# Adding a causal mask in the PSUM bank: identity matmuls on the tensor engine in place of some vector additions

## The chip, the cores and the metric

One core of one Trainium2 chip runs the whole program in one launch. The metric is the device time of one execution, in microseconds (us); the time of a kernel is the median over its runs. All data are float32.

## The reference

The input x holds 8 sequences of 1024 tokens with 256 features. Two layers run over each sequence:

```
x  = x + causal_attention(layernorm(x)) + top1_of_8_experts(layernorm(x))     # layer 0
xn = layernorm(x)
x  = x + attention_on_log_map(xn) + butterfly_ffn(xn)                         # layer 1
```

Both attentions have 16 heads of 16 features. The layer-0 attention is causal:

```python
scores = jnp.einsum('bhki,bhqi->bhkq', k, q) / math.sqrt(HS)
mask = jnp.arange(n)[:, None] <= jnp.arange(n)[None, :]
scores = jnp.where(mask, scores, jnp.float32(NEG_INF))      # NEG_INF = -10000.0
prob = jax.nn.softmax(scores, axis=2)
combined = jnp.einsum('bhkq,bhkl->bhql', prob, v)
```

The layer-1 attention has no mask. The rest (router and experts of layer 0, log map, dynamic metric, butterfly transforms and GELU of layer 1) is not touched here.

## The kernel before

**Naming.** The causal attention of sequence n is called a*n*, the layer-1 attention b*n*; the tiles carry the letter (mx_a, mx_b). The attentions are computed in the order a0, a1, b0, a2, b1, a3, ... a7, b6, b7. An attention is four groups of four heads, and a group has two halves h of 512 query tokens. In a group each head owns a strip of 32 rows of the array, so a score matmul has a contraction of 32 rows and occupies a quarter of the array; the two pairs of heads are called pr = 0 and pr = 1, the two heads of a pair j = 0 and 1.

**Two passes over the scores.** The softmax needs the maximum of each query's row before the exponentials.

- *First pass*, `max_step`: the tensor engine computes scores with the queries on the partitions (L441) into a tile of two PSUM banks, one bank for each head of the pair. The vector engine (DVE) takes the maximum of each row (L455). In a causal attention some 128x128 blocks lie on the diagonal; there DVE first adds `negmask` (0 at and below the diagonal, -1e30 above it) to the scores in the bank (L451). `maxima` (L464 to L475) joins the parts of a half, and `put_max` transposes the negated maxima (L481, tensor engine) and adds them into a free row of the query tile, so that the second pass subtracts them within its matmul.
- *Second pass*, `exp_step` and `weigh`: scores with the keys on the partitions (L504, tensor engine), exponentials (L512, ACT), zeros above the diagonal (L516, POOL), then the products with the values (av, L526, tensor engine, full 128 rows). `norm_out` and `norm` (from L537) divide by the sum, after transposes (tile ut).

**The causal first pass of a group.** A half has, for each pr, one *wide* item with two diagonal blocks (a part 384 wide and a part 128 wide, side by side in the bank) and two *narrow* items with one diagonal block (512 and 256 wide); the second half has four more items without a diagonal. So a group has 4 wide and 8 narrow items with a mask, and the 8 causal attentions have 32 groups, hence 384 additions at L451.

**The order of the work** is written out by a program that runs when the kernel is built; the engines take their instructions in that order. Each step of the main loop issues, for each pr, an `exp_step` of the current group, then as many items of the first pass of a later group as a quota by due time asks for (first the items of the other pr, whose strips of the array are free, so that L441 and L504 run side by side), then the `weigh` of an earlier step, the `norm` and `put_max` that are due, and then fill work. The fill work (projections, router, experts, metric, butterflies, the folded feed-forward with L391 and L1201, layer norms) is given out by a scheduler (`Fill`) from hand-written lanes by planned costs and due times. The planner does not count the time of the mask addition or of anything in `max_step`.

**PSUM.** The tiles of both passes, the transposed maxima (nm) and ut share one ring of three tiles of two banks each (`pair_bank`); av has one bank, the fill work one more.

**Constants.** `ident` (128x128 identity) and `negmask` lie in one constant tile (cst in the profile), both from the host.

Of the kernel before, what the change touches and what calls it, by code (L numbers as in the profile page):

```python
# [18 lines left out]
P = 128  # L19
# [182 lines left out]
def two_layers(ctx: ExitStack, tc: tile.TileContext, a: dict, out: bass.AP):  # L202
# [14 lines left out]
    PE, DVE, ACT, POOL, SP = nc.tensor, nc.vector, nc.scalar, nc.gpsimd, nc.sync  # L217
# [13 lines left out]
    def pair_bank(name):  # L231
        return ps_sc.tile([P, 2, 512], F32, tag="sc", name=name)
# [22 lines left out]
    ident = cst[:, C_ID : C_ID + P]  # L255
    negmask = cst[:, C_NEG : C_NEG + P]
# [29 lines left out]
    for s, tag in enumerate(("gm", "h", "wst", "wst", "second", "xT1", "vT")):  # L286
        bufs = 1 if tag in ("gm", "second", "xT1", "vT") else None
        t = work.tile([P, 2048], F32, tag=tag, name=f"paths_{s}", **({"bufs": bufs} if bufs else {}))
# [34 lines left out]
    for i in range(2):  # L323
        t = const.tile([P, NT, 8, 3, 16], F32, tag=f"vals{i}", name=f"vals{i}")
# [4 lines left out]
    for par in range(2):  # L329
        t = const.tile([P, 4, P], F32, tag=f"negmax{par}", name=f"negmax{par}")  # L330
# [72 lines left out]
    class Attention:  # L403
# [29 lines left out]
        def max_step(self, g, parts, pr):  # L433

            qT, kT, mm = self.q[g], self.k[g], self.mm[g]
            sc = pair_bank(f"mx_{self.n}_{g}_{parts[0][0]}_{parts[0][1]}_{pr}")
            at = [0, parts[0][2]]
            for (t, k, w), o in zip(parts, at):
                for j in range(2):
                    r = 32 * (2 * pr + j)  # L440
                    PE.matmul(  # L441
                        sc[:, j, o : o + w], qT[r : r + 32, t * P : (t + 1) * P],
                        kT[r : r + 32, k * 512 : k * 512 + w], start=True, stop=True,
                    )
            t, k, w = parts[0]
            if self.causal and k * 512 + w == (t + 1) * P:
                shape = [P, 2, len(parts), P]
                own = sc[:, :, w - P : w - P + len(parts) * P].rearrange(
                    "p j (i f) -> p j i f", f=P
                )  # L450
                DVE.tensor_tensor(  # L451
                    own, own, negmask.unsqueeze(1).unsqueeze(1).to_broadcast(shape), ALU.add
                )
            for (t, k, w), o in zip(parts, at):
                DVE.tensor_reduce(  # L455
                    mm[:, t, 2 * pr : 2 * pr + 2, k], sc[:, :, o : o + w], AX.X, ALU.max
                )
# [1138 lines left out]
```

## Time and profile before

| what | value |
|---|---|
| time, median of 3 runs | 4759.27 us (4754.95, 4759.27, 4760.77) |
| profiled execution, own time | 4754.35 us |
| its span | 4752.6 us |
| mean clock granted to the tensor engine | 0.989 |
| busy: tensor engine (PE) | 4596.2 us |
| busy: its weight loads (PEld, beside PE) | 1935.5 us |
| busy: DVE | 3049.0 us |
| busy: ACT | 2206.8 us |
| busy: POOL | 740.8 us |

The profile is one execution as the hardware profiler recorded it. Its span runs from the first to the last instruction; the device time adds 1.75 us. A group line gives line of the kernel, engine, operation, out<-in tiles, their shapes, how many; then busy us, the mean of one in ns, the idle time of the engine just before these instructions, and what ended it. A float32 matmul leaves two records on the tensor engine (and two weight loads), so 2048 matmuls stand as x4096. The end of a matmul is modelled, and matmuls overlap in the pipeline: their mean duration is longer than the distance from one to the next. The chain of waits follows the last instruction back to what released it, step by step. The granted clock is the share of full speed that the tensor engine was given.

In the profile the first pass of a0 lies from 24 to 266 us, that of a1 from 276 to 530 us. Groups 2 and 3 of a2 lie from 1026 to 1144 us, those of a3 from 1610 to 1723, a4 from 2188 to 2300, a5 from 2765 to 2878, a6 from 3343 to 3456 and a7 from 3922 to 4031 us.

### The profile page before, as it was taken

The page shows a single profiled execution, that of the slowest core. Times are in us where ns is not written, and L with a number is a line of the kernel's source. Part 1 is how long each engine was busy: PE and PEld are TensorE (multiplying, and loading weights), DVE is VectorE, ACT ScalarE, POOL GpSimd, SP SyncE. Part 2 cuts the span into 40 slices and gives each one's busy share as a digit, 9 for nine tenths or more (in the row PEclk, how much of TensorE's full clock was granted, in tenths as well). Part 3 has the DMA queues.
Part 4 walks back from the last instruction along what each step waited for, and adds up shares of the span by engine and source line. Part 5 has one row for each costly group of instructions (what it writes and reads, how often), then busy time and mean ns, then how long its engine had stood idle before and what let it go on. Part 6 is the DMA issues. An engine that isn't in the chain of part 4 may idle for free.

```text
span 4752.6 us, 68497 instructions
## 1 busy us (share of the span) xinstructions
PE 4596.2 (97%) x27808; PEld 1935.5 (41%) x27808; DVE 3049.0 (64%) x4926; ACT 2206.8 (46%) x2813; POOL 740.8 (16%) x1213
## 2 busy tenths in 40 slices
PE   7989999999999999999999999999999999999998
PEld 3444443344433444344443444434443344433332
DVE  6777565666566765667656676566675666666554
ACT  2443445544454444544445444454445544454544
POOL 4233202021020210202121021211112011010000
PEclk8899999999999999999999999999999999999999
DMA  4121101020001100012000110001100011000000
GB/s 166 55 66 54 54 3 34 23 67 21 13 25 34 61 18 15 26 34 67 7 27 18 34 62 8 27 22 48 46 6 28 28 40 37 15 10 10 1 10 10
DMA packets 85692, 158.24 MB, mean 33 GB/s; under 512 B 12672, under 2 KB 67584, under 8 KB 82176
## 3 DMA queue, kind: packets, MB, share of 16 engines
q1 hardware_dynamic: 69632, 89.88, 5.7%
q0 software_dynamic: 15744, 63.98, 4.3%
q8 instruction: 219, 3.59, 0.3%
q14 instruction: 97, 0.79, 0.1%
HBM read 117.25 MB, written 36.57 MB: 32 GB/s over the span
## 4 chain that ended last, share of the span: by engine, by line
PE 87%; DVE 7%; ACT 3%; issue 1%; DMA 0%; POOL 0%; POOLq 0%; DVEq 0%; SPq 0%; ACTq 0%
PE sc_b L504 19%; PE av_b L526 10%; PE sc_a L504 9%; PE mx_b L441 6%; PE av_a L526 5%; PE w L1201 5%; PE f L391 5%; PE mx_a L441 4%; PE g_b L1127 2%; PE e L842 2%; DVE mm_a L455 2%; PE h_b L391 2%; ACT p_b L512 2%; PE k_a L391 1%; PE q_b L391 1%
## 5 line engine op out<-in xcount | busy, mean ns | idle before, releaser
L455 DVE TENSOR_REDUCE mm_b<-mx_b 128x2 f32<-128x1024 f32 x1024 | 1249.6, 1223 | 769.6 <-PE mx_b L441 769.1
L512 ACT ACTIVATE p_b<-sc_b 128x1024 f32<-128x1024 f32 x1024 | 1043.0, 1022 | 1184.5 <-PE mx_b L441 740.7
L441 PE MATMUL mx_b<-kT_b,qT_b 32*128 32x512 f32 x4096 | 1144.6, 638 | 10.9 <-ACT p_b L512 10.6
L504 PE MATMUL sc_b<-qT_b,kT_b 32*128 32x512 f32 x4096 | 1142.7, 638 | 9.3 <-ACT p_b L512 6.9
L512 ACT ACTIVATE p_a<-sc_a 128x1024 f32<-128x1024 f32 (+1 forms) x640 | 598.5, 937 | 740.2 <-PE sc_a L504 392.7
L455 DVE TENSOR_REDUCE mm_a<-mx_a 128x2 f32<-128x1024 f32 (+3 forms) x768 | 722.7, 955 | 254.4 <-PE mx_a L441 239.5
L441 PE MATMUL mx_a<-kT_a,qT_a 32*128 32x512 f32 (+3 forms) x3072 | 673.4, 535 | 22.1 <-DVE mm_a L455 15.9
L504 PE MATMUL sc_a<-qT_a,kT_a 32*128 32x512 f32 (+3 forms) x3072 | 679.3, 533 | 8.3 <-ACT p_a L512 5.4
L504 PEld LDWEIGHTS sc_b<-qT_b,kT_b 32*128 32x128 f32 x4096 | 308.7, 183 | 619.7 <-issue 429.9
L526 PE MATMUL av_b<-p_b,vals 128*32 128x512 f32 x4096 | 548.9, 605 | 0.6 <-ACT p_b L512 0.6
L516 POOL TENSOR_SCALAR_AFFINE_SELECT p_a<-p_a 128x256 f32<-128x256 f32 (+1 forms) x384 | 189.4, 493 | 1388.2 <-ACT p_a L512 1387.9
L504 PEld LDWEIGHTS sc_a<-qT_a,kT_a 32*128 32x128 f32 x3072 | 247.0, 186 | 345.5 <-issue 235.1
L441 PEld LDWEIGHTS mx_b<-kT_b,qT_b 32*128 32x128 f32 x4096 | 307.5, 183 | 63.8 <-ACT p_b L512 49.5
L526 PE MATMUL av_a<-p_a,vals 128*32 128x512 f32 (+3 forms) x3072 | 321.3, 507 | 0.0
L451 DVE TENSOR_TENSOR mx_a<-mx_a,cst 128x256 f32<-128x256 f32 (+1 forms) x384 | 198.5, 517 | 174.3 <-PE mx_a L441 131.4
L441 PEld LDWEIGHTS mx_a<-kT_a,qT_a 32*128 32x128 f32 x3072 | 245.2, 187 | 102.6 <-ACT p_a L512 22.8
L1201 PE MATMUL w<-wcon,f 128*128 128x256 f32 x1024 | 260.1, 392 | 3.1 <-ACT f L1193 3.1
L826 POOL DMA_INDIRECT ew<-in_ew,rows_a x120 | 116.7, 973 | 850.3 <-PE mx_b L441 508.6
L526 PEld LDWEIGHTS av_b<-p_b,vals 128*32 128x32 f32 x4096 | 81.1, 108 | 382.3 <-issue 373.6
L1201 PEld LDWEIGHTS w<-wcon,f 128*128 128x128 f32 x1024 | 183.0, 189 | 119.1 <-issue 83.3
L391 PE MATMUL f<-xT_b,wexp 128*128 128x512 f32 x512 | 223.9, 595 | 0.0
L526 PEld LDWEIGHTS av_a<-p_a,vals 128*32 128x32 f32 x3072 | 68.2, 110 | 214.9 <-issue 173.0
(227 smaller groups left out, 4202.9 us busy)
## 6 DMA issues: line engine op xcount, KB each, us to landing
ew<-sorted_d SPq DMA_DIRECT2D x120, 128.0 KB, 2.1
mixed_d<-res SPq DMA_DIRECT2D x120, 128.0 KB, 1.7
x<-in_x SPq DMA_DIRECT2D x8, 1024.0 KB, 5.7
wexp<-wexp_d SPq DMA_DIRECT2D x8, 1024.0 KB, 4.8
wcon<-wcon_d SPq DMA_DIRECT2D x8, 1024.0 KB, 5.4
paths<-in_paths SPq DMA_DIRECT2D x7, 1024.0 KB, 13.3
out<-x SPq DMA_DIRECT2D x7, 1024.0 KB, 4.4
w<-in_w1t SPq DMA_DIRECT2D x8, 512.0 KB, 3.8
```

Of the source, the lines that this page charges most:

```text
L391: PE.matmul(ps, w[:, c, cols : cols + P], rhs[:, c, h * 512 : (h + 1) * 512], start=(c == 0), stop=(c == 1),)
L441: PE.matmul(sc[:, j, o : o + w], qT[r : r + 32, t * P : (t + 1) * P], kT[r : r + 32, k * 512 : k * 512 + w], start=True, stop=True,)
L451: DVE.tensor_tensor(own, own, negmask.unsqueeze(1).unsqueeze(1).to_broadcast(shape), ALU.add)
L455: DVE.tensor_reduce(mm[:, t, 2 * pr : 2 * pr + 2, k], sc[:, :, o : o + w], AX.X, ALU.max)
L504: PE.matmul(sc[:, j, o : o + 512 - c0], kT[r : r + 32, kt * P : (kt + 1) * P], qT[r : r + 32, h * 512 + c0 : (h + 1) * 512], start=True, s ...
L512: ACT.activation(p[:, :, lo:], sc[:, :, lo:], AF.Exp, scale=0.25)
L516: POOL.affine_select(own, own, [[0, 2], [0, n], [1, P]], ALU.is_ge, 0.0, base=0, channel_multiplier=-1,)
L526: PE.matmul(av[32 * i : 32 * i + 32, c0:], self.vals[:, kt, 4 * (g // 2) + i, odd : odd + 2, :].rearrange("p e d -> p (e d)"), p2[i // 2][ ...
L826: POOL.indirect_dma_start(halves[:, s % 2, : 3 * D], None, a["ew"], bass.IndirectOffsetOnAxis(ap=rows[:, s : s + 1], axis=0),)
L842: PE.matmul(ps[:, :D], was[:, c * P : (c + 1) * P], w[:, c * D : (c + 1) * D], start=(c == 0), stop=(c == 1),)
L1127: PE.matmul(ps, w2t[:, m, c * P : (c + 1) * P], hT[:, m, :], start=(m == 0), stop=(m == 3),)
L1201: PE.matmul(ps[:, :D], hT[k // 4][:, k % 4, i * P : (i + 1) * P], wcon[:, k, :], start=(k == 0), stop=(k == 7),)
```

## The change

For all groups of the sequences 0 and 1, and for the groups 2 and 3 of the sequences 2 to 7 (20 of the 32 causal groups), the mask is no longer added by DVE. The score matmul leaves its accumulation open, and for each head j and each diagonal block one more matmul, of `ident` (stationary, 128x128) with `negmask` (moving, 128 columns), adds the mask to the block in the bank: two such matmuls for a narrow item, four for a wide one. They use all 128 rows of the array, in float32 like the others. The groups 0 and 1 of the sequences 2 to 7 keep the addition on DVE. The maximum (L455) is taken as before.

```diff
@@ max_step
             at = [0, parts[0][2]]
+            t, k, w = parts[0]
+            masks = self.causal and k * 512 + w == (t + 1) * P
+            added = masks and (self.b < 2 or g > 1)
             for (t, k, w), o in zip(parts, at):
                 for j in range(2):
                     r = 32 * (2 * pr + j)
                     PE.matmul(
                         sc[:, j, o : o + w], qT[r : r + 32, t * P : (t + 1) * P],
-                        kT[r : r + 32, k * 512 : k * 512 + w], start=True, stop=True,
+                        kT[r : r + 32, k * 512 : k * 512 + w], start=not (o and added), stop=not added,
                     )
             t, k, w = parts[0]
-            if self.causal and k * 512 + w == (t + 1) * P:
+            if added:
+                for j in range(2):
+                    for o in range(w - P, w - P + len(parts) * P, P):
+                        PE.matmul(
+                            sc[:, j, o : o + P], ident, negmask, start=False,
+                            stop=o == w - P + (len(parts) - 1) * P,
+                        )
+            elif masks:
                 shape = [P, 2, len(parts), P]
                 own = sc[:, :, w - P : w - P + len(parts) * P].rearrange(
                     "p j (i f) -> p j i f", f=P
```

## The prediction

> **What bounds the kernel now.** I read the page first, then the chain of waits, then stretches of time, then the groups of the shapes that the change touches, then single moments of the timeline. The page's head and its chain:
>
> ```profile
> span 4752.6 us, 68497 instructions
> ...
> PE 4596.2 (97%) x27808; PEld 1935.5 (41%) x27808; DVE 3049.0 (64%) x4926; ACT 2206.8 (46%) x2813; POOL 740.8 (16%) x1213
> ...
> PE 87%; DVE 7%; ACT 3%; issue 1%; DMA 0%; POOL 0%; POOLq 0%; DVEq 0%; SPq 0%; ACTq 0%
> ```
>
> The tensor engine has work 97% of the time and carries 87% of the chain. A change that moves work from DVE to it starts with a loss, unless it hits the places where DVE is what ends last (7% of the chain, some 330 us). So I asked for the stretches in which the touched mask additions (L451) lie. The first pass of sequences 0 and 1 ends by 560 us; groups 2 and 3 of the sequences 2 to 7 lie in six stretches of about 130 us. Columns: stretch, its length, busy us and instructions of each engine, clock granted to the tensor engine, share of the DMA engines, GB/s.
>
> ```profile
> 0.00:560.00 560.00, 495.22 (x3026) 234.63 (x3028) 414.66 (x840) 220.40 (x322) 176.38 (x282) 0.94 0.25 81
> 1010.00:1140.00 130.00, 122.91 (x754) 55.56 (x752) 84.67 (x159) 54.25 (x67) 24.78 (x45) 0.95 0.15 47
> 1590.00:1720.00 130.00, 123.65 (x792) 55.79 (x788) 88.16 (x166) 56.35 (x69) 25.23 (x47) 0.97 0.14 44
> 2168.00:2298.00 130.00, 123.65 (x803) 55.84 (x795) 89.60 (x169) 56.73 (x70) 25.57 (x48) 0.99 0.14 44
> 2745.00:2875.00 130.00, 123.66 (x794) 55.91 (x788) 88.64 (x166) 56.29 (x69) 25.09 (x47) 0.97 0.14 44
> 3323.00:3453.00 130.00, 122.88 (x796) 55.75 (x788) 88.63 (x166) 56.29 (x69) 25.25 (x47) 0.99 0.14 44
> 3902.00:4032.00 130.00, 125.52 (x814) 56.95 (x812) 84.69 (x148) 57.08 (x70) 23.91 (x47) 1.00 0.11 36
> ```
>
> These 1340 us hold 1237.5 us of tensor work: 102.5 of the 156 us that this engine idles in the whole run are here. 21 of them no mask can touch (13.8 at the start, 7.2 behind one long DVE wait at 37 us). The missing clock is worth another 51 us (0.06 x 560 plus 0.05, 0.03, 0.01, 0.03 and 0.01 x 130). So 81 + 51 = 132 us is what the array loses here to waits and to the half clock that follows them. One such place in the chain, 1066 to 1076 us (start, us, what):
>
> ```profile
> by line: DVE mm_a L455 20.7%; DVE mx_a L451 13.9%; issue 9.9%; PE nm_a L481 8.4%; PE sc_a L504 7.5%; DVE st_a L353 6.6%; DVE on_a L577 4.3%; PE mx_a L441 4.2%; DVE es_a L572 4.2%; DVE mv_a L354 3.6%; DVE negmax L473 3.6%; DVE vals L605 3.3%
> ...
> 1073.26 0.60 DVE mx_a L451
> 1073.86 0.02 issue
> 1073.88 1.30 DVE mm_a L455 x2
> 1075.18 0.14 issue
> 1075.32 0.84 PE nm_a L481 x4
> ```
>
> For 8 us the chain runs on DVE without a break, and the transposes of L481 wait for it.
>
> **What the change removes.** The order of the instructions on ACT, POOL and SP is the same; DVE loses 240 rows, the tensor engine gains 240 groups, and nothing else moves. So the scheduler's plan stays, and the change does what it says.
>
> ```profile
> L451 DVE TENSOR_TENSOR mx_a<-mx_a,cst 128x256 f32<-128x256 f32 x256 | 109.6, 428 | 96.3 <-PE mx_a L441 59.4 <-PE sc_a L504 27.1 <-PE sc_b L504 8.4
> L451 DVE TENSOR_TENSOR mx_a<-mx_a,cst 128x512 f32<-128x512 f32 x128 | 88.9, 695 | 78.0 <-PE mx_a L441 72.0 <-issue 3.0 <-ACT junk_b L1021 2.3
> ```
>
> There are 12 additions in a group (8 narrow, 4 wide), 20 of the 32 groups change: 160 x 0.428 + 80 x 0.695 = 124 us off DVE. How much of it lies on the path? I cut the chain into the seven stretches and read L451's share: 3.9% of the first 560 us (21.8 us) and 3.8 to 4.9% of about 100 us in each of the six (27.5 us together). That is 49 us of the 124, or 39%. The other 61% ran beside tensor work and is worth nothing.
>
> **What it adds.** A narrow item gets two identity matmuls, a wide one four. Each fp32 matmul leaves two records (L441: 2048 for sequences b stand as x4096), so 160 x 4 + 80 x 8 = 1280 records, each 128 columns with a full 128x128 weight load. No such record exists now. The nearest are two moments of the timeline and a group of another shape:
>
> ```profile
> 3594.28 0.30 PEld L684 LDWEIGHTS rank_a<-hot_a,cst 128*128 128x128 f32 x2 [0.76 <-issue]
> 3594.50 0.30 PEld L685 LDWEIGHTS rank_a<-hot_a,ones 128*128 128x128 f32 x2
> 3594.72 1.60 PEld L1201 LDWEIGHTS w<-wcon,f 128*128 128x128 f32 x8
> ```
>
> ```profile
> L391 PE MATMUL f<-xT_b,wexp 128*128 128x512 f32 x512 | 223.9, 595 | 0.0
> ```
>
> Two records of 64 columns follow each other every 0.22 us, 0.11 each. 512 columns cost 223.9 / 512 = 0.437, so 128 columns stream in 0.109. Both ways a record costs 0.11: 1280 x 0.11 = 141 us. A change between full-array and tiled matmuls costs about 0.09 more (L771's neighbour at 2010.41 takes 0.52 until the tiled L504, two records of 256 columns stream in 0.437). In the changed order 140 of the 240 groups stand before a tiled matmul (104 before av, 24 before another mx, 12 before sc), the rest before full-array ones, which only get the change of shape that the mx block pays today: 13 us. Together 154. Bounds: 141 without any such cost; halfway between the 64-column record and the 256-column one of L1201 (260.1 / 1024 = 0.254, so about 0.16), 1280 x 0.16 + 13 = 218. I take 154, since two rows agree on 0.11. It can't be below nothing: the array does these columns in addition.
>
> A rule is weighed here. The Trainium skill, TensorE: Matmul & The Clock Gate, section Back-to-back issue gap, gives about 81 ns for a matmul of 128 columns in a stream of loads and matmuls. By it the records would cost 1280 x 0.081 = 104 us, an estimate from that page, and the whole would end 50 us earlier; the rows above have no full-array record under 0.11.
>
> **What hides.** The identities wait for nothing new: they follow their own item in the same bank. Behind them stand av, the fill work and the next scores, all 0.44 or 0.88 us later. The maximum (L455) now waits for the last identity in place of the addition; 0.44 takes the place of 0.43 and 0.88 that of 0.70, so the bank comes free about when it did where DVE is not late. Where the chain runs on DVE (39% of the touched time) the array waits anyway, and the identities fit in: 0.39 x 154 = 60 us hidden, 94 left. There DVE also gets shorter by 49 us; what is late next is the array itself, with its longer item, so I count two thirds, 33 us. The clock: fewer idle microseconds leave the array at half speed less often; a tenth of 51, 5 us. Sum: 94 - 33 - 5 = +56. Recovered in all: 98 of the 132 us that are there, so I would not go higher.
>
> A second rule speaks against this change: Perfetto Trace Analysis, section Identifying the Most-Contended Engine, says to relieve the engine that is used most, and also that busy matmul time does not measure headroom and the share of weight loads does. By its second half the array, at 41% of weight loads, has room for all 154 us and only DVE's relief would show, 4721 us. The stretches speak against that: the idle time and lost clock there are 132 us, not 59% of 1340.
>
> The profiled execution took 4754.35 us by its own time, 1.75 more than its span; the median of the three runs is 4759.27, 4.9 above. 4754.35 + 56 + 4.9 = 4815.
>
> **The rivals.** *DVE decides the stretches.* The array cools and idles there because DVE is late; the identities fill that time and keep the clock up. All 132 us come back against 141, and DVE's 33 stand: 4754 - 24 = 4730. For it: in 120 to 140 and 160 to 190 us DVE is over 90% busy, the clock under 0.8 in places. Against: even there the chain gives L451 only 39% of its own time. It wins once over 116 us (154 - 33 - 5), three quarters of the identities, are hidden. Chance 0.19. *Nothing hides.* In-order identities push av and the next scores even where DVE was late, and DVE then waits for the array: +154 to +218, 4908 to 4972. For it: 97% busy. Against: the chain above. Chance 0.08. *A draw*, the gain and the loss within 0.2% (9.5 us, about what a measurement of this kernel can tell from no change): 0.07.
>
> **How the numbers follow.** The forecast, slower by 10 to 145 us, has 0.66. Upper end: price 218, 39% of it hidden, 133 left, and little relief, 4890; a piece of the second rival takes it to 4900. Lower end: price 141, hidden 55, the full 49 and half of the clock (25) gives +12; to leave out no more than 2 in 10 the range must reach into the first rival, 4745. Slower 0.66 + 0.08, same 0.07, faster 0.19.
>
> **What would show it.** Right: the new line at about 0.11 us a record, 141 us of full-array work; DVE busy down by 124 to about 2925 us; tensor busy time up by more than the span; idle time and lost clock in the seven stretches down by about 60 to 100 us; sequences' other stretches unchanged in length. Wrong: a record at 0.16 or more; clock and idle time unchanged (then nothing hid); or the stretch 0 to 560 shorter by over 30 us and the six others not longer (then DVE was the bound).

## The result and the profile after

The changed kernel takes 4818.06 us (median of 4 runs, 4812.29 to 4818.78) against 4760.02 us before (4 runs): a ratio of 1.0119, interval 1.0107 to 1.0132. The forecast was 4815 us. The profiled execution has an own time of 4818.13 us.

The page's engine row and chain by engine of the changed kernel:

```profile
span 4816.4 us, 70587 instructions
...
PE 4711.1 (98%) x29088; PEld 2064.1 (43%) x29088; DVE 2927.0 (61%) x4686; ACT 2208.7 (46%) x2813; POOL 740.2 (15%) x1213
...
PE 93%; DVE 3%; ACT 3%; issue 1%; DMA 0%; POOL 0%; POOLq 0%; DVEq 0%; SPq 0%; ACTq 0%
```

DVE is 122 us shorter and its share of the chain falls from 7% to 3%; the tensor engine's rises from 87% to 93%. Its busy time grew by 115 us, the span by 64: its idle time fell by 51.

The group of the identities (line moved to L452) and, from the chain by line, what carries the stretch of groups 2 and 3 of a3, before (1590.53 to 1721.02 us) and after (1617.86 to 1752.80 us; L504, L526, L441 and L455 are now L514, L536, L444 and L465):

```profile
L452 PE MATMUL mx_a<-cst 128*128 128x128 f32 x1280 | 208.4, 296 | 0.0
```

```profile
by line: PE sc_a L504 21.1%; PE av_a L526 11.7%; PE f L391 10.7%; PE mx_a L441 8.3%; issue 7.5%; DVE mm_a L455 5.3%; PE v_b L1087 4.1%; PE k_a L391 3.0%; DVE mx_a L451 2.9%; PE w L1201 2.8%; PE q_a L391 2.8%; ACT p_a L512 2.4%; PE e L842 2.
```

```profile
by line: PE sc_a L514 25.7%; PE av_a L536 14.7%; PE mx_a L452 12.9%; PE mx_a L444 10.7%; PE f L391 10.3%; PE v_b L1097 5.1%; PE k_a L391 2.9%; PE e L852 2.7%; PE w L1211 2.7%; PE q_a L391 2.7%; ACT p_a L522 2.3%; PE nm_a L491 1.7%; PE q_b L
```

Before, `mm_a` and `mx_a` on DVE had 8.2% of this chain; after, they are not among the lines shown, and the identities have 12.9%. Next, the stretches that the prediction showed, each cut at the same ACT instructions in both traces; columns as there. Before, then after, for the first stretch, the one of a3 and the one of a7:

```profile
0.00:559.04 559.04, 494.26 (x3020) 234.50 (x3024) 413.70 (x839) 219.44 (x321) 176.38 (x282) 0.94 0.25 80
1590.53:1721.02 130.49, 124.14 (x788) 55.72 (x781) 88.68 (x166) 56.34 (x69) 25.07 (x46) 0.97 0.14 44
3902.51:4031.82 129.31, 124.83 (x806) 56.59 (x803) 84.05 (x146) 56.90 (x70) 23.75 (x46) 1.00 0.11 37
```

```profile
0.00:579.24 579.24, 542.70 (x3532) 288.86 (x3536) 362.24 (x743) 220.11 (x321) 175.96 (x282) 0.97 0.24 78
1617.86:1752.80 134.94, 133.22 (x907) 67.03 (x900) 77.84 (x144) 56.53 (x69) 25.07 (x46) 1.00 0.13 43
3955.36:4094.99 139.63, 137.39 (x927) 69.08 (x920) 72.85 (x123) 57.06 (x69) 23.75 (x46) 1.00 0.10 34
```

The first stretch is 20.2 us longer, the six late ones 35.5 us together (3.9, 4.4, 6.1, 4.8, 6.0 and 10.3), the others 8 us together; these hold the few identities that lie past the cuts (each late stretch holds 120 to 125 of its 128 records). The stretch of a7 pays most. Before, it had the least to give: 4.5 us idle, clock 1.00, while that of a3, for one, had 6.4 us idle and a clock of 0.97.

Two places of the timeline of the changed kernel (start, us, what) show the price of a group:

```profile
1049.28 1.16 PE L452 MATMUL mx_a<-cst 128*128 128x128 f32 x8
1050.37 1.14 PE L444 MATMUL mx_a<-kT_a,qT_a 32*128 32x384 f32 x8
...
1116.45 0.71 PE L452 MATMUL mx_a<-cst 128*128 128x128 f32 x4
1117.10 1.06 PE L536 MATMUL av_a<-p_a,vals 128*32 128x512 f32 x8
```

Eight records hold the array for 1.09 us, four for 0.65. In the starts of all records the pattern is the same: the first record of a group lasts 0.213 us to the next start, the others 0.111 to 0.112, and the last 0.205 where a tiled matmul follows. Summed over the 240 groups that is 180 us: 1280 x 0.1115 = 143, 240 x 0.10 = 24 for the first records, 140 x 0.093 = 13 for the last ones.

Not all of it is added. A full-array matmul that follows a tiled one has a longer first record too, and loses this when a group of identities stands before it. One place in the changed kernel, then the same place in a kernel of the next section that has no mask there:

```profile
1051.44 1.16 PE L452 MATMUL mx_a<-cst 128*128 128x128 f32 x8
1052.43 1.03 PE L1097 MATMUL v_b<-wv,vT_b 128*128 128x256 f32 x4
```

```profile
1002.70 1.14 PE L444 MATMUL mx_a<-kT_a,qT_a 32*128 32x128 f32 x10
1003.77 1.13 PE L1097 MATMUL v_b<-wv,vT_b 128*128 128x256 f32 x4
```

The four records of L1097 take 1.03 us behind identities and 1.13 behind scores. Over the 100 groups that stand before a full-array matmul these differences sum to about 8 us. So the identities add 172 us of array time. (Taken from the starts at all 240 places in the two kernels, the difference is 169.)

### The profile page after: what moved, and what is told of

Its sections match the earlier page's. It is cut to its first block, busy times and chain, and to the rows that moved or that the text cites. A ratio compares the mean times of both kernels' runs of the same rounds, so it can differ in the third digit from the quotient of the medians.

```text
span 4816.4 us, 70587 instructions
## 1 busy us (share of the span) xinstructions
PE 4711.1 (98%) x29088; PEld 2064.1 (43%) x29088; DVE 2927.0 (61%) x4686; ACT 2208.7 (46%) x2813; POOL 740.2 (15%) x1213
## 4 chain that ended last, share of the span: by engine, by line
PE 93%; DVE 3%; ACT 3%; issue 1%; DMA 0%; POOL 0%; POOLq 0%; DVEq 0%; SPq 0%; ACTq 0%
PE sc_b L514 19%; PE sc_a L514 10%; PE av_b L536 10%; PE mx_b L444 6%; PE av_a L536 6%; PE w L1211 5%; PE f L391 5%; PE mx_a L444 4%; PE mx_a L452 4%; PE g_b L1137 2%; PE e L852 2%; PE h_b L391 2%; ACT p_b L522 2%; PE v_b L1097 1%; PE k_a L391 1%; PE q_b L391 1%
## 5 line engine op out<-in xcount | busy, mean ns | idle before, releaser
L465 DVE TENSOR_REDUCE mm_b<-mx_b 128x2 f32<-128x1024 f32 x1024 | 1249.2, 1222 | 772.0 <-PE mx_b L444 765.6
L444 PE MATMUL mx_b<-kT_b,qT_b 32*128 32x512 f32 x4096 | 1144.7, 638 | 11.4 <-ACT p_b L522 11.2
L514 PE MATMUL sc_b<-qT_b,kT_b 32*128 32x512 f32 x4096 | 1142.6, 638 | 9.2 <-ACT p_b L522 6.8
L465 DVE TENSOR_REDUCE mm_a<-mx_a 128x2 f32<-128x1024 f32 (+3 forms) x768 | 722.0, 954 | 519.1 <-PE mx_a L452 265.3
L444 PE MATMUL mx_a<-kT_a,qT_a 32*128 32x512 f32 (+3 forms) x3072 | 670.0, 527 | 6.9 <-ACT p_a L522 5.5
L514 PE MATMUL sc_a<-qT_a,kT_a 32*128 32x512 f32 (+3 forms) x3072 | 664.8, 524 | 2.5 <-ACT p_a L522 1.3
L514 PEld LDWEIGHTS sc_b<-qT_b,kT_b 32*128 32x128 f32 x4096 | 308.7, 183 | 619.6 <-issue 431.6
L536 PE MATMUL av_b<-p_b,vals 128*32 128x512 f32 x4096 | 548.9, 605 | 0.6 <-ACT p_b L522 0.6
L526 POOL TENSOR_SCALAR_AFFINE_SELECT p_a<-p_a 128x256 f32<-128x256 f32 (+1 forms) x384 | 189.4, 493 | 1457.5 <-ACT p_a L522 1457.2
L514 PEld LDWEIGHTS sc_a<-qT_a,kT_a 32*128 32x128 f32 x3072 | 242.0, 183 | 332.9 <-issue 255.7
L444 PEld LDWEIGHTS mx_b<-kT_b,qT_b 32*128 32x128 f32 x4096 | 307.6, 183 | 66.0 <-ACT p_b L522 51.7
L536 PE MATMUL av_a<-p_a,vals 128*32 128x512 f32 (+3 forms) x3072 | 315.7, 498 | 0.0
L444 PEld LDWEIGHTS mx_a<-kT_a,qT_a 32*128 32x128 f32 x3072 | 243.6, 184 | 72.2 <-ACT p_a L522 21.7
L536 PEld LDWEIGHTS av_b<-p_b,vals 128*32 128x32 f32 x4096 | 81.1, 108 | 382.4 <-issue 373.6
L452 PE MATMUL mx_a<-cst 128*128 128x128 f32 x1280 | 208.4, 296 | 0.0
L452 PEld LDWEIGHTS mx_a<-cst 128*128 128x128 f32 x1280 | 162.4, 192 | 103.5 <-issue 91.1
```

The costliest lines, as they stand in the source:

```text
L444: PE.matmul(sc[:, j, o : o + w], qT[r : r + 32, t * P : (t + 1) * P], kT[r : r + 32, k * 512 : k * 512 + w], start=not (o and added), stop ...
L452: PE.matmul(sc[:, j, o : o + P], ident, negmask, start=False, stop=o == w - P + (len(parts) - 1) * P,)
L465: DVE.tensor_reduce(mm[:, t, 2 * pr : 2 * pr + 2, k], sc[:, :, o : o + w], AX.X, ALU.max)
L514: PE.matmul(sc[:, j, o : o + 512 - c0], kT[r : r + 32, kt * P : (kt + 1) * P], qT[r : r + 32, h * 512 + c0 : (h + 1) * 512], start=True, s ...
L526: POOL.affine_select(own, own, [[0, 2], [0, n], [1, P]], ALU.is_ge, 0.0, base=0, channel_multiplier=-1,)
L536: PE.matmul(av[32 * i : 32 * i + 32, c0:], self.vals[:, kt, 4 * (g // 2) + i, odd : odd + 2, :].rearrange("p e d -> p (e d)"), p2[i // 2][ ...
```

## The experiments

Three explanations give the same sum. **The prediction's**: the identities partly fit into idle time that DVE makes, and DVE's relief gives something besides. **Rival A**: nothing is hidden, and all that comes back is DVE's relief. **Rival B**: the relief is worth nothing, and identities lie in idle time. Each result is compared with the kernel before as it ran on the same chip; it took 4761.7 us there in the runs of the first four, 4749.8 in those of the next four, 4761.8 in those of the last two.

**The price alone.** The addition is kept beside the identities.

```diff
-            elif masks:
+            if masks:
```

> The selected groups get the identity matmuls and keep the addition on DVE as well (the mask is added twice, which changes no maximum of an unmasked score). This shows the price of the identities with DVE not relieved. The prediction's split (154 us of tensor work, 60 of them hidden in idle time that DVE makes, 38 us relief): 4760 + 94 = 4854, 4840 to 4870. Rival A, nothing is hidden and the whole recovery is DVE's relief: 4760 + 154 = 4914, 4900 to 4930. Rival B, DVE's relief is worth nothing and the identities lie in idle time: as with the change, 4818, 4810 to 4830.

Measured: 4865.04, +103 us, ratio 1.0212 (1.0196 to 1.0228). This lies in the prediction's range; A and B are both out. Of the 172 us of added array time 69 took no time, although DVE did as much as before. Taking the addition away from there gives 103 - 58 = 45 us.

**The relief alone.** The mask is left out of the first pass in the selected groups: no identities, no addition (the score matmul closes its accumulation as before), so the maximum is taken over masked scores too and is only an upper bound.

```diff
-            if added:
+            if False:
 ...
-            elif masks:
+            elif masks and not added:
```

> The selected groups get no mask at all in the first pass, neither identities nor addition, so the maximum is taken over the masked scores of the diagonal blocks too. This shows DVE's relief alone. The prediction's split: 4760 - 38 = 4722, 4711 to 4727. Rival A (all of the recovery, 98 us, is relief): 4662, 4650 to 4675. Rival B (relief is worth nothing): 4760, 4750 to 4765.

Measured: 4684.67, -77 us, ratio 0.9832 (0.9817 to 0.9847). All three were wrong: the relief is twice what the prediction gave it, though less than A's. So the parts don't add: +103 and -77 make +26, and both together +58. The other 32 us are time that the identities and the relief both claim, as the table below shows. The first stretch and that of a3 in this kernel:

```profile
0.00:529.78 529.78, 477.86 (x3020) 228.57 (x3024) 365.51 (x744) 219.13 (x322) 176.80 (x282) 0.97 0.26 85
1557.22:1678.74 121.52, 118.63 (x788) 53.85 (x781) 77.72 (x144) 56.54 (x70) 25.53 (x46) 1.00 0.15 47
```

With the same tensor instructions the first stretch is 29 us shorter than before and that of a3 9 us. Idle time and lost clock (1 less the granted clock, times the length; the clock is shown in two digits, so this is good to some 3 us; idle time at half clock, 6 us before and 1 in the change, counts in both columns) over the seven stretches:

| kernel | idle | lost clock |
|---|---|---|
| before | 102.5 | 50.4 |
| identities and addition | 65.7 | 28.4 |
| neither (the relief alone) | 72.8 | 15.9 |
| the change | 50.9 | 17.4 |
| identities twice | 48.3 | 7.7 |

The identities beside the addition bring back 59 of the 153 us in the two columns, the relief alone 64, the change 85: 38 are claimed by both. The relief alone brings 30 us of idle time and 34 of clock. Clock is nearly half of its worth, and the chain of waits doesn't name it under DVE: it shows as longer matmuls (the same 3020 records of the first stretch are busy for 494 us before and 478 without the mask). The tensor engine's waits for `mm_a` on DVE, all of them, before and in the changed kernel (us in total, times, longest):

```profile
PE mx_a L441 <- DVE mm_a L455: 15.9, 22, 1.3
PE ut_a L564 <- DVE mm_a L455: 7.2, 8, 0.9
PE nm_a L481 <- DVE mm_a L455: 5.5, 5, 1.1
PE sc_a L504 <- DVE mm_a L455: 1.5, 4, 0.6
```

```profile
PE mx_a L444 <- DVE mm_a L465: 1.3, 3, 0.7
```

That is 30.1 us before and 1.3 after; without a mask it is 7.4, and with identities and addition 7.6.

**Early and late apart.**

```diff
-            added = masks and (self.b < 2 or g > 1)
+            added = masks and self.b < 2                  # early
+            added = masks and self.b > 1 and g > 1        # late
```

> Identities only in the sequences 0 and 1 (128 of the 240 masked items with two thirds of a microsecond each, the first 560 us). If the stretches do not act on each other: +20 us as in this stretch of the changed kernel's trace, so 4780, 4774 to 4787, and the six late stretches keep their old lengths of 128 to 131 us. If early work pushes what follows (plan and data arrive later): more than 4790.

> Identities only in the groups 2 and 3 of the sequences 2 to 7. If the stretches do not act on each other: +35 us in the six stretches and about 1 us in each stretch between them, 4797, 4790 to 4805; this and the early kernel's difference add up to the change's 58. By the prediction (56 us in proportion to the 112 of 240 items): 4786.

The counts in these texts are wrong: 96 of the 240 items are early and 144 late, so in proportion the late ones would cost 34 us, 4794. Measured: early 4774.60, +13 us (ratio 1.0030, 1.0018 to 1.0042), late 4805.02, +43 us (1.0086, 1.0073 to 1.0100), just past the edge of what was expected. Together 56, as the change within 2 us: the stretches hardly act on each other. In the early kernel the late stretches a3 to a7 keep 129 to 130 us, as expected. By these runs an item costs 0.13 us early and 0.30 late; early, 65 of 559 us were idle at a clock of 0.94. The changed kernel's own trace shows the contrast smaller, +20.2 us early (0.21 an item) and +35.5 in the late stretches (0.25): the first stretch varies from run to run, and is 4.5 us longer than before even in the trace of the late kernel, which doesn't touch it.

**The identities twice.**

```diff
                     for o in range(w - P, w - P + len(parts) * P, P):
+                        for i in range(2):
                             PE.matmul(
                                 sc[:, j, o : o + P], ident, negmask, start=False,
 ...
```

> The changed kernel with each identity matmul issued twice in a row (the mask is added twice), 1280 records more and nothing else. This shows the marginal price once the idle time is used up. If a record costs 0.11 us and the idle time of the touched stretches is mostly spent (37 + 15 us are left in the changed kernel's seven stretches, 21 of them at places no mask can touch): 4818 + 143 less up to 25 hidden, 4950, 4936 to 4963. Rival: still 39% is hidden, 4818 + 87 = 4905, 4895 to 4915. Rival: a record costs 0.16 or more: over 5000.

Measured: 4945.77, ratio 1.0411 (1.0394 to 1.0428), +196 us. The second 1280 records cost 196 - 58 = 138 us, 0.108 each. This is as expected: the first ones had used up nearly all that could be hidden.

**All groups.**

```diff
-            added = masks and (self.b < 2 or g > 1)
+            added = masks
```

> Identities in all 32 causal groups, no addition left on DVE: 768 records more than in the changed kernel, in stretches in which the tensor engine idles 6 of 450 us at full clock. If only idle time hides them: 768 x 0.11 + 9 for changes of shape = 93, less 6 (the share of the addition in the chain there): 4818 + 87 = 4905, 4893 to 4913. Rival: hidden and relieved as in the selected groups, 58 x 144 / 240 = 35: 4853, 4840 to 4866.

Measured: 4885.45, +136 us, ratio 1.0287 (1.0270 to 1.0304), 78 more than the change, 0.54 us an item. Neither expectation met it: it is 20 us below the first one (4905) and 32 above the rival's. An item costs over twice the selected groups' 0.24 (58 / 240), so the selection took the cheaper ones. The same 144 groups stand 107 us in the array, of which the matmuls behind them get back 6; of the 101 added, 23 came back. The last experiment but one gives 13 of them to DVE. The idle time outside the seven stretches falls by only 4 us from the changed kernel (54 to 50). The other 10 us are not explained; the interval is 8 us to each side.

**A cheaper identity.** Identity and mask as bf16 copies.

```diff
+    mask16 = const.tile([P, 2 * P], mybir.dt.bfloat16, tag="mask16", name="mask16")
+    POOL.tensor_copy(mask16, cst[:, : 2 * P])
+    ident16, negmask16 = mask16[:, :P], mask16[:, P:]
 ...
-                            sc[:, j, o : o + P], ident, negmask, start=False,
+                            sc[:, j, o : o + P], ident16, negmask16, start=False,
```

> The changed kernel with the identity and the mask as bf16 copies (made once by POOL at the start), so one record for each identity matmul in place of two. No trace shows a bf16 record: bounds 0.055 (half of the float32 record) and 0.11 each, 640 of them, 35 to 70 us and 13 for shapes, 48 to 83 in place of 154. The kernel with identities and addition together showed 103 us for the identities alone, so some 51 were hidden, and 47 of relief when the addition goes. With these: 4762 - 47 + (0 to 32) = 4715 to 4747, take 4730. Rival: a change of type in the stream costs as much as is saved, or the record is no shorter and no fewer: 4800 to 4820.

Measured: 4707.92, ratio 0.9909 (0.9893 to 0.9926), -42 us. Its group and a moment of its timeline:

```profile
L455 PE MATMUL mx_a<-mask 128*128 128x128 bf16 x640 | 77.8, 224 | 0.0
```

```profile
1014.61 0.28 PE L455 MATMUL mx_a<-mask 128*128 128x128 bf16 x2
1014.73 0.61 PE L577 MATMUL ut_a<-cst,u_a 128*128 128x128 f32 x4
```

There is one record for each matmul and it lasts 0.056 us, so a matmul costs a quarter: 0.056 beside 2 x 0.1115. Two hold the array for 0.12 us where four float32 records, at a place like this one, hold it for 0.55. All 240 groups stand 52 us. The same idea with the same place wins, because this price is less than the 77 us that the relief alone is worth: 35 of the 52 show beside the kernel without a mask. How much of the bf16 identities would be hidden without the relief was not run.

**No mask in any group** (`added = masks` in the kernel of the relief alone).

> No mask in the first pass of any causal group: neither identities nor additions; the maximum is taken over the masked scores of the diagonal blocks too, and so is an upper bound of the one needed. The kernel that did this in the 20 selected groups took 4685. If the addition costs time only where DVE is late: 4685 less about 6 (its share of the chain elsewhere), 4679, 4668 to 4684. Rival: DVE's relief is worth the same in every group, 77 x 144 / 240 = 46 more: 4639, 4625 to 4655.

Measured: 4660.22, -90 us, ratio 0.9809 (0.9792 to 0.9825). That is 13 us more than without a mask in the selected groups, where 6 and 46 were expected: the additions that the change left on DVE cost little. This is the fastest kernel here. Its maximum bounds the scores from above; with other inputs, where a masked score exceeds the largest unmasked one of its row by far, the exponentials would underflow.

**bf16 in all groups, and the bf16 kernel beside it.**

> The bf16 identities in all 32 causal groups, no addition on DVE. The bf16 kernel gave 42 us below the kernel before, and its 240 groups of identities stand 52 us from their first record to the next other one. For 144 more: 31 us, less the 13 by which the kernel without any mask is below the one without a mask in the selected groups, less a few hidden: 5 to 18 above the bf16 kernel, so 24 to 37 below the kernel before, take 31 (4729 beside 4760). Rival: every group gains like the selected ones, 42 x 384 / 240 = 67 below.

> The bf16 kernel again, on the same chip as the kernel with bf16 identities in all groups, so that the two can be compared. 42 us below the kernel before, 36 to 48.

Measured: 4719.39, ratio 0.9912 (0.9896 to 0.9929), and 4715.87, ratio 0.9904 (0.9887 to 0.9921). They are 42 and 46 us below the kernel before. At this price the selection hardly matters: 3.5 us more (4718 to 4721 beside 4714 to 4717), where 5 to 18 were expected and the rival had 67 below.

## Why the prediction was right

**The sum.** It was +56, and +58 was measured. Its parts, in us:

| step | predicted | measured | from |
|---|---|---|---|
| array time that the identities add | 154 | 172 | starts of the records: 180, less 8 behind them |
| hidden | 60 | 69 | identities beside the addition: 172 - 103 |
| relief and clock | 38 | 45 | 103 - 58 |
| sum | +56 | +58 | |

Each part is of the right kind and somewhat too small; 18 more cost and 16 more recovery cancel. The hit within 3 us is partly luck.

**The price.** The record at 0.11 was right (0.111 to 0.112). The term that was mis-sized is the change of shape: the text charged only the way out, before tiled matmuls (140 groups, 13 us, as measured), and took the way in as paid already. That is so for the 100 groups before a full-array matmul, which no longer pays its own way in. For the 140 before a tiled one the 0.10 of the first record is new, 14 us; the other 4 are the record (0.1115 for 0.11) and what the 100 don't get back in full. The bound of 0.16, called halfway between 0.11 and 0.254, should have been 0.18; and the price by the 81 ns, 104 us, is 37 below the 141 of the same records, not 50. The text also said that no full-array record of 128 columns exists in the trace of before. That was wrong; the matmul of L850 has this shape (240 records, 277 ns mean; their starts lie 0.109 us apart), and would have been the nearest row.

**What hides.** The step "39% of the touched time is DVE's, so 39% of the identities are hidden" gave 60; 69 of 172 are 40%. That DVE's lateness left the room is shown by the kernel without a mask, where the tensor engine's waits for `mm_a` fall from 30.1 to 7.4 us and the clock rises; that the room is limited, by doubling: the second set found next to nothing. The step's share was read for the additions and applied to the identities, an average over places that differ.

**The relief.** Two thirds of 49 us plus a clock term of 5 came out near the 45 only because the identities had already taken part of it. As a statement about DVE alone it failed: 49 us, the addition's share of the chain, was taken as "the full" gain, and without a mask the selected groups give 77. When the addition goes, the tensor engine waits less for the reductions behind it, 23 us less, and the array regains 34 us of clock; the prediction gave the clock a tenth of 51.

**The rivals.** "Nothing hides" is refuted by +103 against 172. "DVE decides the stretches" needed three quarters of the identities to be hidden, 116 us; 69 were. Its outcome, a gain, came with the bf16 identities, whose price is lower than the relief. The rule that the tensor engine's headroom is read from its weight loads, which the prediction weighed, would have given 4721; the stretches decided rightly against it.

**The marks.** DVE at 2927.0 us (about 2925 was said); tensor busy time up by 115, more than the span; idle time and lost clock down from 153 to 68 us, 85 (60 to 100 was said); the other stretches longer by 1 to 2 us, partly from identities past the cuts. Of the 114 us that came back (172 - 58) these 85 are seen as idle time and clock; the other 29 lie in time that the view counts as busy, and what they are stays open.

## What to carry to other kernels

Moving work from an engine that is late in places to one that is busy everywhere is priced by two numbers: what the added work adds to the array's time (beside the same kernel without it: 8 of the 180 us at the new line were only moved there from the next), and how much idle time and lost clock the place has; only what fits into the second is free, and the relief competes for the same time. Measure the two sides apart (add without removing, remove without adding) before judging the idea, since their effects don't add. If the place is right and the price too high, look for a cheaper form of the same step: the identity and the mask in bf16 turned +58 us into -42, and the first question, whether the step is needed at all, was worth -90.

## What the runs showed of the hardware

- A full-array float32 matmul that follows a 32-row one holds its first record 0.10 us longer: 0.213 us in place of 0.111 at 128 columns (the identities), 0.320 in place of 0.218 at 256 (`v_b`, without and with identities before it). A bf16 identity at the same place shows 0.066 and 0.056, but the first float32 record of `v_b` behind it lasts 0.272. Whether it is the change of shape or the weight load that costs this is open.
- A bf16 matmul of 128 columns costs 0.056 us in one record, the float32 one 0.223 in two. The Trainium skill, FP8 and Floating Point Precision, section TensorE Precision Notes, gives true float32 four passes through the array; the ratio here, 4.0, agrees.
- The Trainium skill, TensorE: Matmul & The Clock Gate, section Back-to-back issue gap, gives about 81 ns for a matmul of 128 columns in a stream. Here, in groups of two to eight records, a float32 record takes 111 to 112 ns and a bf16 record 55 to 56; neither is at 81.
- Taking work from DVE gave more (77 us) than that work's share of the chain (49 us).
